# RWKV6 block on one core: one pool of six large tiles, squares of the head norm laid side by side, and a new planned order

## The chip, the core and the metric

The kernel runs on one core of a Trainium2 chip, all in float32. A core has the engines TensorE (PE: matmuls, and its weight loads PEld), VectorE (DVE), ScalarE (ACT), GpSimd (POOL) and SyncE (SP), which here issues nearly all DMAs. Each engine works through its own queue in order; engines wait for each other by semaphores. The metric is the device time of one execution in microseconds, the median of several runs.

## The reference

One RWKV6 block for B=32 sequences of L=128 tokens with E=512 channels, as H=32 heads of S=16. Cut to what matters:

```python
xn = _ln(x, ln1_w, ln1_b)
sx = _token_shift(xn, state[:, i1])                     # previous token minus this one
xxx = jnp.tanh((xn + sx * maa_x) @ maa_w1).reshape(b, l, 5, 1, EXTRA_MAA)
xxx = jnp.matmul(xxx, maa_w2).reshape(b, l, 5, E)
x5 = xn[:, :, None] + sx[:, :, None] * (maa_stack + xxx)  # five mixes: k, w, v, r, g
w = jnp.exp(-jnp.exp(time_decay + jnp.tanh(x5[:, :, 1] @ decay_w1) @ decay_w2))
r, k, v = x5[:, :, 3] @ Wr.T, x5[:, :, 0] @ Wk.T, x5[:, :, 2] @ Wv.T   # as (b, l, H, S)
g = jax.nn.silu(x5[:, :, 4] @ Wg.T)
def step(s, rkvw):                                      # scan over the 128 tokens, s: (b, H, S, S)
    a = k_t[:, :, :, None] * v_t[:, :, None, :]
    out = jnp.einsum('bhk,bhkd->bhd', r_t, u * a + s)
    return (a + w_t[:, :, :, None] * s, out)
a4 = att.reshape(b, l, H, S)                            # norm over each head's 16 values
att = ((a4 - m) * jax.lax.rsqrt(var + EPS)).reshape(b, l, E) * gn_w + gn_b
x = x + att * g @ Wo.T
xn2 = _ln(x, ln2_w, ln2_b)
xk, xr = xn2 + sx2 * ffn_maa_k, xn2 + sx2 * ffn_maa_r
return x + jax.nn.sigmoid(xr @ ffn_Wr.T) * (jnp.square(jax.nn.relu(xk @ ffn_Wk.T)) @ ffn_Wv.T)
```

## The kernel before

The 32 sequences are worked in nine groups, g0 to g8, of 2, 4, 4, 4, 4, 4, 4, 4 and 2. A group has a **front** (layernorm, token shift, the five mixes, the projections w, k, r, v, g), a **recurrence** and a **back** (head norm, gate, Wo, second layernorm, the FFN with its weights Fk, Fr, Fv). The work of several groups overlaps: TensorE does the front of a later group and the back of an earlier one while VectorE and GpSimd run the recurrence between them.

The order is not written in the program text. Each piece of work is a generator (a stream) that yields one operation at a time, with its engine, a guessed cost in microseconds, what it reads and writes, and the tiles it allocates. `Plan` (L101 to L207) runs when the kernel is built. It keeps a clock for each engine, takes of all streams those whose next operation can start within `EPSILON` (L49) of the earliest, and emits the one that is most due. Due times come from the table `DUE` (L53 to L77): for each kind of stream a start and an end in units of groups. So the guessed costs, `DUE` and `EPSILON` fix the order of each engine's queue, and the chip then follows that order whatever the true durations are. A tile name has a number of buffers (the spec, L228 to L242), and an allocation waits until a buffer of that name has been let go (`end=`).

The streams that matter here:

- Front: `front_mix` (L426; L439 and L442 make the shift, `mixed` L466 to L480 the five mixes with L470 and L475 on VectorE, L472 on GpSimd, after the L424 matmuls), `front_proj` (L510; the projections are the L407 matmuls, evicted by `k_out` L556, `r_out` L565 and `v_out` L576, and stored to DRAM by `store` L516, DMA L524), `front_gate` (L626; L642, L644, store L646), `front_state` (L648; its reduce L656).
- Recurrence, for each sequence in eight units: GpSimd multiplies k and v (L723) and adds pairs (L727); ACT copies the decay (L700) and the state (L711); VectorE scans (L742) and multiplies by r (L744); PE sums (L761). POOL makes the bonus (L772, L775, L779). VectorE adds both into y (L790). y has one buffer for a whole group; `rec_out` allocates it anew for a group's first sequence. vL, wL, rL, kL are loads from DRAM by SP (L679, L687), v2 too (L683).
- Back (L802): ACT squares y (L812), VectorE sums a head's 16 squares (L815), takes the reciprocal root in small steps (L818 to L825, three Newton steps) and scales y (L827). SP moves y in 16 DMAs into yc, the layout for matmuls (L835), loads the gate (L841); ACT applies the norm's weights (L843), VectorE the gate (L850), PE multiplies by Wo (L857). VectorE adds x and takes sums (L866), then layernorm in `layernorm_T` (L340: squares L364, L367, POOL L369, L371, L374, transposes L394, L384), the two mixes (L873, L876; L886, L888), Fk (L407 matmuls) with squared relu on ACT into kk (L913, L915), Fr (L923) with a sigmoid on ACT (L935), Fv (L938), VectorE (L928, L930) and the store of the result by SP (L932).

Large tiles of four by 512 floats a partition come under several names: "mx" (three buffers: the mixes, att), "ev" (one buffer: in turn the normalized x of both layernorms where they need one, the squares of y, yc and kk), "wch" and "pk" (one each, decay and k of the front). The two forms of the squares' layout are written in L810 to L815:

```python
sqv = sq.t.rearrange("p e n -> p (e n)")[:, 0 : S * nb * TC].rearrange("p (s m) -> p s m", s=S)
yv = y.t.rearrange("p s b c -> p s (b c)")[:, :, 0 : nb * TC]
nc.scalar.activation(sqv, yv, AF.Square)
...
nc.vector.tensor_reduce(m2, sqv.rearrange("p s m -> p m s"), AX.X, ALU.add)
```

Here m counts sequence and token (128 of them in a group of four), s the 16 values of a head. The squares lie as y does, s outermost, so the sum over s steps over m: 512 bytes in a group of four.

## Time and profile before

| | us |
|---|---|
| median of 3 runs | 1525.69 (1522.88, 1525.69, 1531.78) |
| the profiled execution | 1523.82, its span 1522.0 |
| busy PE | 1333.5 (88% of the span) |
| busy DVE | 1198.4 (79%) |
| busy POOL | 1084.2 (71%) |
| busy ACT | 633.7 (42%) |
| L815, the reduce of a group of four | 3.692 each, 7 of them |
| L812, the squares of a group of four | 1.911 each, 7 of them |
| L742 and L744, a unit of the recurrence on VectorE | 1.223 and 1.219 each, 256 of each |
| mean granted clock of TensorE | 0.932 |

The profile is one execution on the chip, taken by the hardware profiler. Its first part gives each engine's busy time. Its slices cut the span in 40 equal parts of 38 us; each digit is the busy share in tenths, and PEclk is the share of full speed that TensorE's clock was granted. A group line reads: line of the kernel, engine, operation, output tile <- input tiles, shapes, count, then busy us and mean ns of one, then idle time of the engine just before and what ended it. A line of waits reads: who waited, for whom, us in total, how often, longest. In a timeline, a line begins with start and duration in us, and the bracket gives idle time before it with the releaser. SPq stands for SP issuing DMAs.

### The profile page before, as it was taken

What the parts mean: (1) busy time and instruction counts of PE and PEld (TensorE: products, weight loads), DVE (VectorE), ACT (ScalarE), POOL (GpSimd) and SP (SyncE); (2) the same over time, 40 slices, a digit from 0 to 9 for tenths busy, and PEclk for the clock granted to TensorE, in tenths of its full rate; (3) what the DMA queues carried; (4) which work ended last, traced back from release to release, by engine and by line L of the source; (5) the groups of instructions that cost most, each with busy time, mean ns of one, the idle gap of its engine ahead of it and who ended that gap; (6) DMA issues with size and microseconds to landing.
All of it is one profiled execution on the core that took longest, in us unless ns stands there. A gap on an engine that the chain in (4) does not pass through costs nothing.

```text
span 1522.0 us, 18535 instructions
## 1 busy us (share of the span) xinstructions
PE 1333.5 (88%) x6060; PEld 606.3 (40%) x6060; DVE 1198.4 (79%) x1600; ACT 633.7 (42%) x1358; POOL 1084.2 (71%) x747
## 2 busy tenths in 40 slices
PE   8979988988899997999899998999899929955947
PEld 7734433442344333443344433443344506312413
DVE  4679788889788888779798898899888877886221
ACT  3433433453356422663255423653265314523413
POOL 3069569896889758795779867986898759977000
PEclk9989998998999998999999998999899969977979
DMA  5542736464655256553655366635565355535131
GB/s 186 166 111 106 216 105 189 147 173 127 187 157 162 84 151 185 166 159 103 187 180 175 86 177 214 186 98 155 167 184 161 102 141 152 160 88 161 39 89 65
DMA packets 292065, 222.52 MB, mean 146 GB/s; under 512 B 103936, under 2 KB 227840, under 8 KB 290816
## 3 DMA queue, kind: packets, MB, share of 16 engines
q1 hardware_dynamic: 291424, 221.10, 48.8%
q8 instruction: 48, 0.79, 0.2%
q14 instruction: 49, 0.40, 0.1%
q10 hardware_dynamic: 544, 0.23, 0.1%
HBM read 165.71 MB, written 47.19 MB: 140 GB/s over the span
## 4 chain that ended last, share of the span: by engine, by line
PE 58%; DVE 16%; issue 9%; SPq 6%; POOL 4%; DMA 4%; ACT 2%; POOLq 0%; DVEq 0%; ACTq 0%
PE ps L407 26%; PE ps L923 6%; PE ps L938 6%; PE ps L857 5%; PE acc L761 5%; SPq L835 4%; PE ps L424 4%; DVE sc L742 3%; DVE rm L744 3%; POOL am L723 2%; PE ps L413 2%; PE ps L394 1%; PE ps L450 1%; DVE mx L470 1%; DVE th L815 1%
## 5 line engine op out<-in xcount | busy, mean ns | idle before, releaser
L723 POOL TENSOR_TENSOR am<-vL,kL 128x1024 f32<-128x1024 f32 x256 | 604.0, 2360 | 70.9 <-DMA vL<-dv 53.2
L407 PE MATMUL ps<-mx,wt 128*128 128x512 f32 (+1 forms) x1440 | 591.5, 561 | 18.3 <-DVE mx L477 4.2
L407 PEld LDWEIGHTS ps<-mx,wt 128*128 128x128 f32 x1440 | 268.2, 193 | 304.8 <-issue 240.5
L742 DVE TENSOR_TENSOR_SCAN sc<-sc,a 128x512 f32<-128x512 f32 x256 | 313.1, 1223 | 31.0 <-POOL a L727 26.3
L727 POOL TENSOR_TENSOR a<-am 128x504 f32<-128x504 f32 x256 | 263.3, 1028 | 102.9 <-DVE sc L742 88.5
L744 DVE TENSOR_TENSOR rm<-sc,rL 128x1024 f32<-128x1024 f32 x256 | 312.2, 1219 | 14.4 <-PE acc L761 4.4
L700 ACT COPY sc<-wL 128x512 f32<-128x512 f32 x256 | 150.8, 589 | 257.6 <-DVE rm L744 250.7
L761 PE MATMUL acc<-rm,sel 128*32 128x256 f32 x2048 | 152.5, 408 | 61.5 <-DVE rm L744 61.4
L857 PE MATMUL ps<-wt,mx 128*128 128x512 f32 x256 | 123.3, 639 | 45.0 <-DVE mx L850 37.7
L472 POOL TENSOR_TENSOR mx<-mx,xnT 128x512 f32<-128x512 f32 (+1 forms) x96 | 105.2, 1113 | 68.6 <-DVE mx L470 68.1
L711 ACT COPY a<-st 128x8 f32<-128x8 f32 x256 | 51.5, 204 | 185.4 <-DVE sc L742 181.4
L761 PEld LDWEIGHTS acc<-rm,sel 128*32 128x32 f32 x2048 | 54.4, 112 | 171.6 <-DVE rm L744 82.4
L938 PE MATMUL ps<-wt,ev 128*128 128x512 f32 x256 | 117.6, 602 | 0.3 <-DVE mx L477 0.3
L923 PE MATMUL ps<-wt,mx 128*128 128x512 f32 x256 | 116.5, 598 | 0.6 <-ACT wch L539 0.4
L369 POOL TENSOR_TENSOR rstd<-rstd,mhalf 128x4 f32<-128x4 f32 (+1 forms) x18 | 17.1, 948 | 120.3 <-DVE rstd L367 119.9
L857 PEld LDWEIGHTS ps<-wt,mx 128*128 128x128 f32 x256 | 51.4, 206 | 114.6 <-issue 57.7
L424 PE MATMUL ps<-tha,w2p 64*128 64x512 f32 (+1 forms) x288 | 86.5, 624 | 10.0 <-DVE blk L644 4.3
L475 DVE SCALAR_TENSOR_TENSOR ps<-ps,vec,sx 128x512 f32<-128x512 f32 (+1 forms) x84 | 55.6, 662 | 23.6 <-PE ps L424 23.3
L938 PEld LDWEIGHTS ps<-wt,ev 128*128 128x128 f32 x256 | 46.7, 190 | 62.7 <-issue 50.7
L923 PEld LDWEIGHTS ps<-wt,mx 128*128 128x128 f32 x256 | 47.4, 190 | 60.7 <-issue 52.4
L470 DVE SCALAR_TENSOR_TENSOR mx<-ps,vec,sx 128x512 f32<-128x512 f32 (+1 forms) x96 | 65.5, 706 | 5.7 <-PE ps L424 5.7
L928 DVE SCALAR_TENSOR_TENSOR ps<-th,ps 128x512 f32<-128x512 f32 x32 | 22.1, 689 | 53.7 <-PE ps L938 37.0
(108 smaller groups left out, 1413.0 us busy)
## 6 DMA issues: line engine op xcount, KB each, us to landing
vL<-dv SPq DMA_DIRECT2D x128, 256.0 KB
x<-in_x SPq DMA_DIRECT2D x14, 1024.0 KB
wt<-in_wk SPq DMA_DIRECT2D x9, 1024.0 KB
wt<-in_wr SPq DMA_DIRECT2D x9, 1024.0 KB
wt<-in_wg SPq DMA_DIRECT2D x9, 1024.0 KB
wt<-in_wo SPq DMA_DIRECT2D x9, 1024.0 KB
wt<-in_fk SPq DMA_DIRECT2D x9, 1024.0 KB
wt<-in_fr SPq DMA_DIRECT2D x9, 1024.0 KB
```

Source lines behind the costliest of these rows:

```text
L407: nc.tensor.matmul(p[:, cols], lhsT=w[:, c, e * P : (e + 1) * P], rhs=xin[:, c, cols], start=(c == 0), stop=(c == NE - 1))
L424: nc.tensor.matmul(p[:, cols], lhsT=w[h, :], rhs=t[h, cols], start=True, stop=True)
L472: nc.gpsimd.tensor_tensor(bt(x5[:, f, cols]), bt(x5[:, f, cols]), row(xnT, f, 1, nb), ALU.add)
L700: nc.scalar.copy(sc.t, w[:, q : q + 1, :].to_broadcast([P, DH, T2]))
L723: nc.gpsimd.tensor_tensor(am.t, v[:, ds, :], k[:, q : q + 1, :].to_broadcast([P, DH, L]), ALU.mult)
L727: nc.gpsimd.tensor_tensor(a[:, :, 1:T2], am2[:, :, 0 : T2 - 1, 0], am2[:, :, 0 : T2 - 1, 1], ALU.add)
L742: nc.vector.tensor_tensor_scan(scf, scf, a.t.rearrange("p d n -> p (d n)"), 0.0, ALU.mult, ALU.add)
L744: nc.vector.tensor_tensor(pair(rm.t), sc.t.unsqueeze(3).to_broadcast([P, DH, T2, 2]), r2[:, q : q + 1, :, :].to_broadcast([P, DH, T2, 2]), ...
L761: nc.tensor.matmul(acc[j * H : (j + 1) * H, dh * DH * TC : (dh + 1) * DH * TC].rearrange("p (d c) -> p d c", c=TC), lhsT=sel, rhs=rm[:, :, ...
L857: nc.tensor.matmul(p.t, lhsT=att[:, c, b * L : (b + 1) * L], rhs=wot[:, c, :], start=(c == 0), stop=(c == NE - 1))
L923: nc.tensor.matmul(p.t, lhsT=xr[:, c, b * L : (b + 1) * L], rhs=frt[:, c, :], start=(c == 0), stop=(c == NE - 1))
L938: nc.tensor.matmul(p2.t, lhsT=kk[:, c, b * L : (b + 1) * L], rhs=fvt[:, c, :], start=(c == 0), stop=(c == NE - 1))
```

## The change

Three things change.

1. The names "ev", "wch" and "pk" go, and "mx" has six buffers in place of three. Six large tiles exist before and after; now any stream's large tile takes any of them. The allocations that named the three now name "mx" (in `layernorm_T`, `decay`'s first tile, the k projection, the squares, yc and kk).
2. The squares are written with a head's 16 values side by side: ACT's output now steps by 16 floats (64 bytes) from one value to the next, and the reduce reads adjacent values.
3. The planner gets other numbers: guessed costs of the stores (0.65 to 0.4), of L835 (2.6 to 2.9 for four DMAs) and of the second and third part of the bonus (0.65 to 0.72), another `EPSILON` and another table `DUE`. A mix is handed on when all four of its parts are made, in whatever order, in place of after the second half. No operation is added or taken out; the order of each queue is found anew.

```diff
--- before.py
+++ after.py
@@ -46,34 +46,34 @@
 LANDING = 2.0
 HOP = (0.2, 0.05, 0.05, 0.04, 0.08)
 ON_POOL = (2, 3, 4)
-EPSILON = 0.2067
+EPSILON = 0.1801
 
 
 OWN = {("mix", "first"), ("mix", "second"), ("mix", "last"), ("proj", "first"), ("proj", "second"), ("proj", "last"), ("weights", "first"), ("weights", "second"), ("gate", "first"), ("gate", "last"), ("back", "last"), ("back", "late"), ("back", "first")}
 DUE = {
-    "back": (0.998, 2.47),
-    "back_last": (-18.697, 1.751),
-    "back_late": (-42.476, -38.604),
-    "gate_last": (-7.141, -59.547),
-    "mix": (-2.339, -1.036),
-    "proj": (-1.408, -0.356),
-    "proj_second": (-1.35, 0.093),
-    "rec": (0.043, 8.058),
-    "weights": (-40.47, -7.934),
...
+    "back": (0.996, 2.471),
+    "back_last": (8.448, 60.13),
+    "back_late": (-31.956, -8.84),
+    "gate_last": (4.32, -85.128),
+    "mix": (-2.222, -1.037),
+    "proj": (-1.486, -0.286),
+    "proj_second": (-23.559, 1.139),
+    "rec": (0.042, 8.059),
+    "weights": (-72.983, -42.3),
...
 }
 
 
@@ -228,8 +228,8 @@
     spec = [
         (big, [P, GB, E], "x", 2), (big, [P, NE, E], "wt", 3),
         (big, [P, NE * GB, L + 1], "xnT", 1), (big, [P, NE, N], "sx", 1),
-        (big, [P, NE, N], "mx", 3), (big, [P, NE, N], "ev", 1), (big, [P, N], "blk", 4),
-        (big, [P, NE, N], "wch", 1), (big, [P, NE, N], "pk", 1), (big, [P, NE, N // 2], "pa", 1),
+        (big, [P, NE, N], "mx", 6), (big, [P, N], "blk", 4),
+        (big, [P, NE, N // 2], "pa", 1),
         (big, [P, Q, T2], "wL", 2), (big, [P, Q, L], "rL", 2), (big, [P, Q, L], "kL", 2), (big, [P, S, L], "vL", 2),
         (big, [P, S, TC], "v2", 1), (big, [P, S, TC + TC // 2], "bo", 1), (big, [P, GB, TC + TC // 2], "rk", 2),
         (big, [P, S, GB, TC], "y", 1), (big, [P, GB, Q, S], "st", 2),
@@ -358,7 +358,7 @@
             xh = None
             for b in bs:
                 if xh is None:
-                    (xh,) = yield Op(ACT, 0.83, r=[(src, b), (mv, "m")], w=[(0, b), (mv, ("v", b))], alloc=["ev"])
+                    (xh,) = yield Op(ACT, 0.83, r=[(src, b), (mv, "m")], w=[(0, b), (mv, ("v", b))], alloc=["mx"])
                 else:
                     yield Op(ACT, 0.83, r=[(src, b), (mv, "m")], w=[(xh, b), (mv, ("v", b))])
                 nc.scalar.activation(xh[:, b, :], src[:, b, :], AF.Square, bias=mv[:, b, 0:1],
@@ -476,7 +476,7 @@
                     yield Op(DVE, part(0.69, nb), r=[(p, None), (xnT, None)], w=[(x5, f)], end=[p])
                     nc.vector.tensor_tensor(bt(x5[:, f, cols]), bt(p[:, cols]), row(xnT, f, 1, nb), ALU.add)
                 d["mixed", m, f] = True
-            if i == 1:
+            if all(("mixed", m, f) in d for f in range(NE)):
                 d["x5", m] = x5
 
         for m in (1, 0, 3, 2, 4):
@@ -516,10 +516,10 @@
         def store(name, src, f, width, end):
             rows = slice(f * P, (f + 1) * P)
             if f == 0:
-                (d[name],) = yield Op(SP, 0.65, r=[(src, None)], w=[(0, f)], alloc=[name], xfer=part(1.2, nb), end=end)
+                (d[name],) = yield Op(SP, 0.4, r=[(src, None)], w=[(0, f)], alloc=[name], xfer=part(1.2, nb), end=end)
             else:
                 yield Op(SP, 0.0, need=lambda: name in d)
-                yield Op(SP, 0.65, r=[(src, None)], w=[(d[name], f)], xfer=part(1.2, nb), end=end)
+                yield Op(SP, 0.4, r=[(src, None)], w=[(d[name], f)], xfer=part(1.2, nb), end=end)
             t = src.t.rearrange("p b n -> p (b n)") if name == "dw" else src.t
             nc.sync.dma_start(out=d[name].t[rows, 0:width], in_=t[:, 0:width])
 
@@ -545,7 +545,7 @@
                 d["w", f] = True
 
         for i in range(2):
-            pp = yield Op(PE, PAIR * pe, r=[(dlo, None)], w=[(0, None), (1, None)], alloc=["ps", "ps"] + ([] if i else ["wch"]),
+            pp = yield Op(PE, PAIR * pe, r=[(dlo, None)], w=[(0, None), (1, None)], alloc=["ps", "ps"] + ([] if i else ["mx"]),
                           end=[dlo] if i else [])
             if i == 0:
                 wch = pp.pop()
@@ -578,7 +578,7 @@
             nc.scalar.copy(ev[:, cols], p[:, cols])
             yield from store("dv", ev, f, n, [ev])
 
-        for m, name, evict, take in ((0, "k", k_out, ["pk"]), (3, "r", r_out, ["pa"]), (2, "v", v_out, [])):
+        for m, name, evict, take in ((0, "k", k_out, ["mx"]), (3, "r", r_out, ["pa"]), (2, "v", v_out, [])):
             yield Op(PE, 0.0, need=lambda: ("x5", m) in d and ("w", name) in d and (m != 2 or "centered" in data[0]))
             x5, w = d["x5", m], d["w", name]
             late = []
@@ -770,11 +770,11 @@
             (bo,) = yield Op(POOL, 1.25, r=[(v2, None), (rk, None)], w=[(0, 0)], alloc=["bo"], port=True)
             one, two = bo[:, :, 0:TC], bo[:, :, TC : TC + TC // 2]
             nc.gpsimd.tensor_tensor(one, v2.t, rk[:, b : b + 1, 0:TC].to_broadcast([P, S, TC]), ALU.mult)
-            yield Op(POOL, 0.65, r=[(v2, None), (rk, None)], w=[(bo, 1)], port=True,
+            yield Op(POOL, 0.72, r=[(v2, None), (rk, None)], w=[(bo, 1)], port=True,
                      end=[v2] + ([rk] if b == SIZES[g] - 1 else []))
             nc.gpsimd.tensor_tensor(two, v2.t.rearrange("p s (m j) -> p s m j", j=2)[:, :, :, 0],
                                     rk[:, b : b + 1, TC : TC + TC // 2].to_broadcast([P, S, TC // 2]), ALU.mult)
-            yield Op(POOL, 0.65, r=[(bo, 1)], w=[(bo, 0)], port=True)
+            yield Op(POOL, 0.72, r=[(bo, 1)], w=[(bo, 0)], port=True)
             odd = one.rearrange("p s (m j) -> p s m j", j=2)[:, :, :, 1]
             nc.gpsimd.tensor_tensor(odd, odd, two, ALU.add)
             unit[i, "bo"] = bo
@@ -806,13 +806,13 @@
         yield Op(DVE, 0.0, need=lambda: "rec" in d and ("gate", NE - 1) in d)
         y = d["y"]
         wot = yield from weight(wo, lambda: g < 1 or ("back", "weights") in data[g - 1])
-        (sq,) = yield Op(ACT, part(1.9, nb), r=[(y, b) for b in bs], w=[(0, None)], alloc=["ev"])
-        sqv = sq.t.rearrange("p e n -> p (e n)")[:, 0 : S * nb * TC].rearrange("p (s m) -> p s m", s=S)
+        (sq,) = yield Op(ACT, part(1.9, nb), r=[(y, b) for b in bs], w=[(0, None)], alloc=["mx"])
+        sqv = sq.t.rearrange("p e n -> p (e n)")[:, 0 : S * nb * TC].rearrange("p (m s) -> p m s", s=S)
         yv = y.t.rearrange("p s b c -> p s (b c)")[:, :, 0 : nb * TC]
-        nc.scalar.activation(sqv, yv, AF.Square)
+        nc.scalar.activation(sqv.rearrange("p m s -> p s m"), yv, AF.Square)
         (small,) = yield Op(DVE, part(2.3, nb), r=[(sq, None)], w=[(0, None)], alloc=["th"], end=[sq])
         m2, yy, t = (small[:, i * P : i * P + nb * TC] for i in range(3))
-        nc.vector.tensor_reduce(m2, sqv.rearrange("p s m -> p m s"), AX.X, ALU.add)
+        nc.vector.tensor_reduce(m2, sqv, AX.X, ALU.add)
 
         yield Op(DVE, part(0.69, nb), w=[(small, None)], port=True)
         nc.vector.tensor_scalar(m2, m2, 1.0 / S, EPS, ALU.mult, ALU.add)
@@ -828,9 +828,9 @@
         yc = None
         for e in range(NE):
             if yc is None:
-                (yc,) = yield Op(SP, 2.6, r=[(y, None)], w=[(0, e)], alloc=["ev"], xfer=part(1.6, nb))
+                (yc,) = yield Op(SP, 2.9, r=[(y, None)], w=[(0, e)], alloc=["mx"], xfer=part(1.6, nb))
             else:
-                yield Op(SP, 2.6, r=[(y, None)], w=[(yc, e)], xfer=part(1.6, nb), end=[y] if e == NE - 1 else [])
+                yield Op(SP, 2.9, r=[(y, None)], w=[(yc, e)], xfer=part(1.6, nb), end=[y] if e == NE - 1 else [])
             for j in range(Q):
                 nc.sync.dma_start(out=yc[:, e, j * nb * TC : (j + 1) * nb * TC],
                                   in_=yv[j * H + e * HE : j * H + (e + 1) * HE])
@@ -907,7 +907,7 @@
             if e > 0:
                 p, f = late.pop(0), e - 1
                 if kk is None:
-                    (kk,) = yield Op(ACT, part(0.6, nb), r=[(p, None)], w=[(0, f)], alloc=["ev"], end=[p])
+                    (kk,) = yield Op(ACT, part(0.6, nb), r=[(p, None)], w=[(0, f)], alloc=["mx"], end=[p])
                 else:
                     yield Op(ACT, part(0.6, nb), r=[(p, None)], w=[(kk, f)], end=[p])
                 nc.scalar.activation(kk[:, f, cols], p[:, cols], AF.Relu)
```

"..." in the table stands for its other rows, which all change as well.

More of the change, by code (lines that the diff above doesn't have):

```diff
@@ L48 @@
 ON_POOL = (2, 3, 4)
-EPSILON = 0.2067
+EPSILON = 0.1801
 OWN = {("mix", "first"), ("mix", "second"), ("mix", "last"), ("proj", "first"), ("proj", "second"), ("proj", "last"), ("weights", "first"), ("weights", "second"), ("gate", "first"), ("gate", "last"), ("back", "last"), ("back", "late"), ("back", "first")}
 DUE = {
-    "back": (0.998, 2.47),
-    "back_first": (1.001, 2.842),
-    "back_last": (-18.697, 1.751),
-    "back_late": (-42.476, -38.604),
-    "center": (18.233, -20.613),
-    "gate": (5.025, -13.659),
-    "gate_first": (-1.137, -8.429),
-    "gate_last": (-7.141, -59.547),
-    "load": (-12.908, 19.489),
-    "mix": (-2.339, -1.036),
-    "mix_first": (1.194, 5.467),
-    "mix_last": (-11.53, -12.113),
-    "mix_second": (-1.924, -0.827),
-    "proj": (-1.408, -0.356),
-    "proj_first": (-2.407, -0.516),
-    "proj_last": (-9, 3.206),
-    "proj_second": (-1.35, 0.093),
-    "rec": (0.043, 8.058),
-    "state": (4.949, 0.89),
-    "warm0": (30.81, 39.251),
-    "weights": (-40.47, -7.934),
-    "weights_first": (16.502, 1.704),
-    "weights_second": (-22.418, -15.321),
+    "back": (0.996, 2.471),
+    "back_first": (1.379, -4.163),
+    "back_last": (8.448, 60.13),
+    "back_late": (-31.956, -8.84),
+    "center": (62.31, -1.713),
+    "gate": (4.863, -6.444),
+    "gate_first": (-0.774, -0.627),
+    "gate_last": (4.32, -85.128),
+    "load": (-6.043, -5.031),
+    "mix": (-2.222, -1.037),
+    "mix_first": (3.302, -4.409),
+    "mix_last": (-11.933, -1.779),
+    "mix_second": (-3.08, -0.718),
+    "proj": (-1.486, -0.286),
+    "proj_first": (-12.879, -4.085),
+    "proj_last": (-18.756, -7.148),
+    "proj_second": (-23.559, 1.139),
+    "rec": (0.042, 8.059),
+    "state": (0.71, -1.021),
+    "warm0": (2.516, 64.442),
+    "weights": (-72.983, -42.3),
+    "weights_first": (16.549, 19.386),
+    "weights_second": (-13.091, 8.817),
 }
```

## The prediction

> **What bounds the kernel now.** I read the page's slices first, then the waits of each engine, then the tail (1405 us to the end) engine by engine.
>
> ```profile
> PE   8979988988899997999899998999899929955947
> POOL 3069569896889758795779867986898759977000
> PEclk9989998998999998999999998999899969977979
> ```
>
> Up to slice 32 (38 us each) TensorE is the bound: one period of a middle group (L450 of one group to the next) is 163 to 179 us. From slice 33 on the fronts run out, PE falls to 2, later to 5, 5 and 4, and first the recurrence on POOL and VectorE sets the pace (POOL 9, 9, then 7, 7), then, with POOL empty, a chain that no engine's throughput bounds.
>
> ```profile
> PE ps L857 <- DVE mx L850: 21.2, 1, 21.2
> PE ps L394 <- ACT ev L374: 5.0, 2, 4.7
> ...
> 1453.40 0.60 ACT L935 ACTIVATE th<-ps 128x512 f32<-128x512 f32 x1 [6.27 <-PE ps L923]
> 1456.84 1.06 ACT L812 ACTIVATE ev<-y 128x1024 f32<-128x1024 f32 x1 [2.84 <-PE ps L938]
> 1469.26 0.57 ACT L843 ACTIVATE ps<-ev,vec 128x256 f32<-128x256 f32 x1 [11.37 <-DMA ev<-y]
> ...
> 1464.45 10.37 SPq L835 DMA_DIRECT2D ev<-y  x16
> ```
>
> These are the waits of PE after 1400 us and the timelines of ACT and SP. The last y (L790) is written at 1409.33, the last sums (L761) end at 1409.2. Yet its squares (L812) start at 1456.84, 47 us later, released by PE's last L938. The cause is in the names: L812 writes tile "ev", which has one buffer, and kk of the group before (g7) sits in it until that group's last L938. Only then follow L815, Newton's steps and L827 (to 1464.38), 16 transfers one after another on SP (10.37 us), L843, L850, and L857 at 1477.96: 21.2 us of idle PE, and a cold one afterwards (granted clock 0.59 between 1457 and 1478).
>
> **The change part by part**, against the profiled run (1523.82 us: span 1522.0 and 1.8 around it; 1.9 under the median 1525.69).
>
> *Squares side by side (L810 to L815).* No instruction is added or removed. L815 now reads 16 adjacent values in place of values 512 bytes apart; L812 now writes with a step of 64 bytes.
>
> ```profile
> L815 DVE TENSOR_REDUCE th<-ev 128x128 f32<-128x2048 f32 x7 | 25.8, 3692 | 0.0
> L656 DVE TENSOR_REDUCE stats<-st 128x16 f32<-128x256 f32 x7 | 2.8, 405 | 0.0
> L656 DVE TENSOR_REDUCE stats<-st 128x8 f32<-128x128 f32 x2 | 0.6, 279 | 0.0
> L812 ACT ACTIVATE ev<-y 128x2048 f32<-128x2048 f32 x7 | 13.4, 1911 | 0.0
> L812 ACT ACTIVATE ev<-y 128x1024 f32<-128x1024 f32 x2 | 2.1, 1053 | 2.8 <-PE ps L938 2.8
> ```
>
> L656 is a reduce over 16 adjacent values: (405-279)/128 = 0.98 ns an element and 0.15 us fixed. So 2048 elements: 2.17 us in place of 3.69, 1024: 1.16 in place of 1.90. That is 7 x 1.52 + 2 x 0.74 = 12.1 us of VectorE. In the chain of the whole run L815 stands with its 3.5 us four times (364, 548, 1220, 1351 us), elsewhere it is beside PE work. So 4 x 1.5 = 6, at most 12. L812 costs 0.84 ns an element; no row shows ACT writing 2048 elements strided. From below: ACT's small strided writes, L711 (8 elements 256 bytes apart, 204 ns) and L378 (16, 516 bytes apart, 209 ns), show no price for the step, so 0. From above: the step costs ACT what it costs VectorE's reads, 1.80-0.98 = 0.82 ns an element from L815 and L656, 1.7 us each, and eats the gain. I take 0, nearest to the ACT rows, less a little: **-5**, bounds -12 and +3.
>
> The Trainium skill (SBUF — State Buffer, section "Door 1: The DMA port swizzle") speaks against this edit: full bandwidth needs at least two hits in a 16-byte line, so float32 with a step of four or more pays at each element. The 0.8 ns on L815's read agrees; for ACT's write no row here shows it. By the rule, as an estimate, the sum of this edit would be about 0 instead of -5.
>
> *Six shared tiles, costs, due times, EPSILON.* None of these adds an instruction; they move buffers and the order of each engine's queue, fixed when the kernel is built. I compared both orders. In groups 2 to 5 TensorE's sequence is nearly the same, L812 still stands behind all L935 of the back before it, the L835s stay where they were. So the middle gains nothing but the reduce: **0**, bounds -2 and +2 us at each of 7 boundaries. Three places differ.
>
> *(a) Start.* The state loads go ahead of x on SP (two issues, about +1 us), k and r mixing is interleaved otherwise, the four v projections stand together, and the first vL may load some us earlier (before: v stored by 70.1, but the vL issue at 77.14 queued behind the gate's store; POOL's first L723 at 84.99). **-3**, bounds -6 and +1.
>
> *(b) When the last recurrence ends.* DVE's queue from g7's last y to the last L744 holds more in the new order: L876 x4 and L888 x4 (4 x 0.78 x 2 = 6.2 us) and some L928/L930 now stand before the last L744, and L815 to L827 as before. Against that, one stall goes:
>
> ```profile
> 1375.66 1.22 DVE L744 TENSOR_TENSOR rm<-sc,rL 128x1024 f32<-128x1024 f32 x1
> 1383.44 0.69 DVE L790 TENSOR_TENSOR y<-acc,bo 128x512 f32<-128x512 f32 x1 [6.56 <-DMA ev<-y]
> ```
>
> L790 of g8 writes y, whose one buffer is free when g7's 16 transfers have read it. They took 19 us after L827; only 12.6 us of VectorE work stood between L827 and this L790, now 26. The stall goes and nothing else is late there: the next wait is L850's, on the same transfers, as now. Also g7's L812 stands ahead of the last three L935s of g6 and L815 only 3 us of VectorE work after the last y (before: 11 us, with L815 at 1350.66, y at 1338.09). The same stall one group earlier (6.54 at 1252.12) has 16.6 us of work in place of 13.7 to hide it: -3. I sum rows along both DVE queues: g7's last y comes 5.4 us of work earlier, the stretch from it to the last L744 grows by 11.6 us of work, less 1.5 (reduce): -5.4 + 11.6 - 1.5 - 6.6 - 3 = -5. The L876s add a wait on VectorE: behind each stand recurrence steps, and PE's L761 waits for those. From the first L850 to the first L876 it took 28 us before (1384.2 to 1412), and only 25 us of VectorE work stand between them now: 2 to 3 us of waiting, up to 10 if each L876 waits (17.9 us for ACT in 14 places). Sum: -5 + 3 = **-2**, bounds -15 (the boundary chain 10 us earlier, no waits) and +10.
>
> *(c) The tail.* Before, from the last L761 (1409.2) to the span's end: 112.8 us. In the new order g7's four L407 groups (4 x 3.48 = 14 us) stand ahead of the last L761, L812 ahead of all four L935 of g7, and DVE runs L790, L815 to L827 before the first L928. After the last L761 PE has:
> - g7's L923 and L938, four pairs of 3.43 + 3.43: 27.5 us;
> - a gap before L857, below;
> - from L857's start to the end as before 1522.0-1477.96 = 44.0, less 2.0 because L857 now starts warm (16 took 8.81 us; 16 at L923's 3.43 per 8 take 6.86).
>
> The gap: the chain now runs beside the 27.5 us. L790 0.7, L812 1.06, L815 1.16, then Newton to L827's end (1464.38-1458.24-1.85 = 4.3) is done 7.3 us after the last L761. L835's 16 issues and L841 took 12.4, landing to L850 3: about 23 in all. But SP's new order mixes g7's four output stores (L932) between the L835s: 4, store, 8, store, 4 and one L841, store, three L841, store. The n-th store waits for L930 after the n-th L938, 8.3, 15.2, 22.0 us after the last L761. So the third store holds the last three gate loads until 22, they land by 25.5, and the fourth L850 waits anyway for the fourth L928/L930: 27.5 + 1.4 + 0.4. The gap is 2 us, not 21.2. Also behind the last store now: x and two weight loads of the last group, some 2 us later against L857 than before (issued 1476.80 to 1478.3); L866 needs x 7 us after L857's start and L407 its weight 16 after: covered, and if not, 2 us.
> Sum: 27.5 + 2 + 42 = 71.5 against 112.8: **-41**, bounds -43 and -28 (gap 15, if SP holds the L835s a pair longer twice).
>
> **Sum:** -5 + 0 - 3 - 2 - 41 = -51; 1522.0 - 51 + 1.8 = 1473 us.
>
> **Rivals.**
> 1. *The tail's chain stays late.* If L827 ends over 3 us later than I count, each block of L835 falls behind the next store, and a pair (6.9 us) is lost per block, two at most: +14. For it: 16 issues at 0.65 us fit the gaps of 6.9 us with little to spare. Against: the first four need only be issued before 8.3. 1487 us.
> 2. *The recurrence pays.* FFN work moved ahead of the last steps delays them: the L876s and L888s stall VectorE in order, the last sums move by +10, the start and the reduce give nothing: 1523.8 - 41 + 10 = 1493.
> 3. *The tail does not do what it says.* A front or back tile holds the sixth buffer, or L812 still waits for g7's L938; only the reduce and the start stay: 1516. Against it: no buffer is asked for by a front any more at that point.
> 4. *Slower: the shared pool at the boundaries.* Now kk, normalized x, squares, yc, mixes and projections take any of six buffers in the planned order; a tile of the back planned into a buffer that in truth comes free late stalls PE at each of the 7 middle boundaries, where a stretch of 40 us now loses 6.9 us of PE (33.1 busy, granted clock 0.93, 720 to 760 us). It decides from 51/7 = 7.3 us a boundary, a doubling of this lull. At 9 us: 1473 + 63 = 1536. For it: before, two idle stretches of 6 to 7 us at L424 and L857 already come from such waits (L424 <- L850 20.0 us in 3). Against: in groups 2 to 5 PE's order is nearly the same.
>
> **How the numbers follow.** Forecast (1455 to 1482) 0.55; rival 1 0.12, rival 2 0.12, rival 3 0.07, rival 4 0.09; better than forecast (boundary chains earlier everywhere) 0.05. Range: low end start -6, reduce -12, recurrence -12, tail -43: 1523.8 - 73 = 1451; the high end takes in rivals 1 and 2 and goes half-way from 2 to 3: 1506. About 0.5% (8 us) is what a measurement here can tell from no change; rival 3 lies at its edge. Faster 0.85, same 0.06, slower 0.09.
>
> **What would show it.** Right: L812 of the last group within 3 us of the last L761; no PE wait over 5 us before the last L857; from the last L761 to the end 70 to 75 us; L815 at 2.2 us, L812 at 1.9; no DVE wait at the last group's first L790; L450 of groups 2 to 5 spaced as before. Wrong: L812 at 3.5 us; SP's L835 in the tail waiting for L938; the last L744 later than 1410; a boundary where PE idles 10 us or more.

## The result and the profile after

The changed kernel takes 1475.66 us (median of 4 runs, 1474.92 to 1479.69), the kernel before 1526.24 on the same chip; the ratio is 0.967 with a 95% interval of 0.964 to 0.970. The forecast was 1473. The profiled execution has a span of 1477.9 us against 1522.0: 44.1 us less. The number was met; two of the steps behind it were not, and their errors cancelled, which is luck. What follows shows both.

The slices of the page after (36.9 us each), the same three rows as shown of before:

```profile
PE   7979998998799998999899998999899985676997
POOL 3069568997889779896889878896889957987300
PEclk8989999999889998999999999999999996787998
```

The 2 that stood in slice 33 of before is gone, and the last two slices are a 9 and a 7 where a 4 and a 7 stood: TensorE works to the end.

The tail of the changed kernel, from the timelines of ACT, SP and PE:

```profile
1406.90 0.63 ACT L915 ACTIVATE mx<-mx 128x512 f32<-128x512 f32 x1
1408.03 1.95 ACT L812 ACTIVATE mx<-y 128x1024 f32<-128x1024 f32 x1 [0.50 <-DVE y L790]
...
1415.55 2.69 SPq L835 DMA_DIRECT2D mx<-y  x4
1418.34 0.41 SPq L932 DMA_DIRECT2D out<-x  x1
1418.79 5.34 SPq L835 DMA_DIRECT2D mx<-y  x8
1424.23 0.41 SPq L932 DMA_DIRECT2D out<-x  x1
...
1431.31 3.60 PE L938 MATMUL ps<-wt,mx 128*128 128x512 f32 x8
1434.74 7.03 PE L857 MATMUL ps<-wt,mx 128*128 128x512 f32 x16
1446.41 0.48 PE L394 MATMUL ps<-ident,mx 128*128 128x128 f32 x1 [4.64 <-ACT mx L374]
```

L812 of the last group waits for the last y (0.5 us) and for nothing else. SP mixes L835 and L932 as forecast, and no store holds a transfer for long. L857 follows the last L938 without a gap (no bracket behind it) and runs warm, that is at a higher granted clock (1.00, before 0.80): 7.03 us in place of 8.81. From the end of the last L761 (1407.2) to the end it takes 70.7 us; 71.5 was forecast, 112.8 was before.

The squares and their reduce, by shape, after:

```profile
L812 ACT ACTIVATE mx<-y 128x2048 f32<-128x2048 f32 x7 | 26.1, 3722 | 0.4 <-DVE y L790 0.4
L815 DVE TENSOR_REDUCE th<-mx 128x128 f32<-128x2048 f32 x7 | 16.0, 2283 | 8.5 <-ACT mx L812 8.5
```

The reduce fell from 3692 to 2283 ns (2170 was forecast), but L812 rose from 1911 to 3722 ns, and VectorE now waits for it. The pair takes 6.00 us in place of 5.60.

**Where the 44.1 us came from.** Both are the profiled executions; that of the changed kernel is the slowest of its four. I cut both spans at the last y of a group (L790's timeline):

| from, to | before | after | difference |
|---|---|---|---|
| start to g1's last y | 345.7 | 347.1 | +1.4 |
| g1's to g2's | 175.1 | 167.5 | -7.6 |
| g2's to g3's | 179.8 | 164.4 | -15.4 |
| g3's to g7's | 637.5 | 634.4 | -3.1 |
| g7's to the end | 183.9 | 164.5 | -19.4 |

So 23 us come off between g1's last y and g3's, for which nothing but the reduce was forecast. The following lines, busy time by stretch (start, end, length, then PE, its weight loads, VectorE, ACT and POOL, each with its number of instructions, and the granted clock), show the stretches g1 to g2, g2 to g3, g3 to g4 and g4 to the end, first of before:

```profile
345.70:520.80 175.10, 162.67 (x705) 67.20 (x705) 151.09 (x194) 78.09 (x164) 138.75 (x93) 0.95 0.50 151
520.80:700.60 179.80, 165.04 (x699) 69.22 (x699) 148.96 (x189) 77.56 (x162) 135.90 (x92) 0.94 0.49 147
700.60:866.00 165.40, 157.16 (x697) 67.06 (x696) 144.03 (x188) 76.47 (x161) 134.70 (x91) 0.98 0.54 160
866.00:1522.00 656.00, 543.60 (x2391) 245.51 (x2389) 487.34 (x643) 260.24 (x555) 442.74 (x301) 0.90 0.47 137
```

and of after:

```profile
347.10:514.60 167.50, 152.75 (x672) 63.99 (x670) 140.89 (x182) 77.63 (x160) 138.02 (x92) 0.94 0.52 155
514.60:679.00 164.40, 157.79 (x697) 66.70 (x696) 144.45 (x187) 78.34 (x160) 136.95 (x91) 0.97 0.55 161
679.00:843.10 164.10, 156.96 (x697) 66.49 (x696) 144.03 (x187) 78.36 (x161) 136.95 (x91) 0.98 0.55 161
843.10:1477.90 634.80, 549.63 (x2391) 248.90 (x2389) 490.47 (x643) 267.87 (x555) 447.05 (x301) 0.92 0.48 141
```

A last y is not the same point of PE's queue in both kernels. From g1 to g2 the changed kernel has 33 matmuls less (672 against 705) and more idle PE (14.8 us against 12.4); it has done 36 of them before g1's last y (1608 against 1572), where its PE idles 32.8 us in place of 40.6. So this stretch is shorter because work of it was done earlier, in what was idle time of the start, though the table shows +1.4 there. At g2's last y both have done nearly the same matmuls (2280 and 2277), and the changed kernel is 6.2 us ahead. At g4's the same 2391 are left in both: from g2 to g4 it gains 16.7 us, from there to the end 21.2.

From g3 to g5 both kernels have the same period, 164 to 165 us. Before gets there one group later: its stretch g2 to g3 has as many matmuls as the next one (699 against 697), but 14.8 us of idle PE against 8.2, and the same matmuls take 165.0 us against 157.2, at a clock of 0.94 against 0.98. Half of the long stretch's idle time is one wait that the changed kernel doesn't have there:

```profile
PE ps L424 <- DVE pk L573: 7.5, 1, 7.5
```

Here 6.6 us more of idle PE went with 7.9 us more for the same matmuls, at the lower clock. That the idle time lowered the clock is read from the two together; no run separates them.

### The profile page after: what moved, and what is told of

The parts are those of the page before. It is cut to its first block, busy times and chain, and to the rows that moved or that the text cites. A ratio compares the mean times of both kernels' runs of the same rounds, so it can differ in the third digit from the quotient of the medians.

```text
span 1477.9 us, 18571 instructions
## 1 busy us (share of the span) xinstructions
PE 1331.5 (90%) x6060; PEld 607.9 (41%) x6060; DVE 1185.8 (80%) x1600; ACT 647.3 (44%) x1358; POOL 1094.6 (74%) x747
## 4 chain that ended last, share of the span: by engine, by line
PE 58%; DVE 16%; issue 8%; POOL 6%; SPq 5%; DMA 5%; ACT 3%; POOLq 0%; DVEq 0%; ACTq 0%
PE ps L407 26%; PE ps L923 6%; PE ps L938 6%; PE acc L761 5%; PE ps L424 5%; PE ps L857 4%; DVE sc L742 4%; POOL am L723 3%; SPq L835 3%; DVE rm L744 3%; PE ps L394 2%; POOL a L727 2%; DMA blk<-dgate 2%; PE ps L413 2%; PE ps L450 1%
## 5 line engine op out<-in xcount | busy, mean ns | idle before, releaser
L723 POOL TENSOR_TENSOR am<-vL,kL 128x1024 f32<-128x1024 f32 x256 | 605.3, 2365 | 45.9 <-DMA vL<-dv 17.1
L407 PE MATMUL ps<-mx,wt 128*128 128x512 f32 (+1 forms) x1440 | 590.3, 561 | 9.9 <-DVE mx L470 3.1
L407 PEld LDWEIGHTS ps<-mx,wt 128*128 128x128 f32 x1440 | 271.0, 195 | 290.5 <-issue 237.3
L744 DVE TENSOR_TENSOR rm<-sc,rL 128x1024 f32<-128x1024 f32 x256 | 311.9, 1218 | 14.6 <-PE acc L761 5.8
L761 PE MATMUL acc<-rm,sel 128*32 128x256 f32 x2048 | 153.0, 409 | 90.4 <-DVE rm L744 90.1
L472 POOL TENSOR_TENSOR mx<-mx,xnT 128x512 f32<-128x512 f32 (+1 forms) x96 | 115.2, 1216 | 68.0 <-DVE mx L470 67.7
L761 PEld LDWEIGHTS acc<-rm,sel 128*32 128x32 f32 x2048 | 52.2, 111 | 204.2 <-DVE rm L744 96.7
L711 ACT COPY a<-st 128x8 f32<-128x8 f32 x256 | 51.8, 203 | 180.0 <-DVE sc L742 179.3
L938 PE MATMUL ps<-wt,mx 128*128 128x512 f32 x256 | 122.7, 624 | 7.6 <-DMA wt<-in_fv 7.6
L857 PE MATMUL ps<-wt,mx 128*128 128x512 f32 x256 | 122.5, 639 | 3.7 <-ACT th L935 3.7
L923 PE MATMUL ps<-wt,mx 128*128 128x512 f32 x256 | 116.5, 598 | 0.0
L424 PE MATMUL ps<-tha,w2p 64*128 64x512 f32 (+1 forms) x288 | 81.4, 602 | 6.1 <-ACT mx L539 4.2
L857 PEld LDWEIGHTS ps<-wt,mx 128*128 128x128 f32 x256 | 51.9, 206 | 73.4 <-issue 59.0
L938 PEld LDWEIGHTS ps<-wt,mx 128*128 128x128 f32 x256 | 48.5, 197 | 73.1 <-issue 53.1
L923 PEld LDWEIGHTS ps<-wt,mx 128*128 128x128 f32 x256 | 47.5, 190 | 61.1 <-issue 52.8
L384 ACT ACTIVATE xnT<-ps,vec 128x512 f32<-128x512 f32 (+1 forms) x72 | 52.5, 729 | 15.8 <-PE ps L394 15.7
```

Of the source, the lines that this page charges most:

```text
L407: nc.tensor.matmul(p[:, cols], lhsT=w[:, c, e * P : (e + 1) * P], rhs=xin[:, c, cols], start=(c == 0), stop=(c == NE - 1))
L424: nc.tensor.matmul(p[:, cols], lhsT=w[h, :], rhs=t[h, cols], start=True, stop=True)
L472: nc.gpsimd.tensor_tensor(bt(x5[:, f, cols]), bt(x5[:, f, cols]), row(xnT, f, 1, nb), ALU.add)
L723: nc.gpsimd.tensor_tensor(am.t, v[:, ds, :], k[:, q : q + 1, :].to_broadcast([P, DH, L]), ALU.mult)
L744: nc.vector.tensor_tensor(pair(rm.t), sc.t.unsqueeze(3).to_broadcast([P, DH, T2, 2]), r2[:, q : q + 1, :, :].to_broadcast([P, DH, T2, 2]), ...
L761: nc.tensor.matmul(acc[j * H : (j + 1) * H, dh * DH * TC : (dh + 1) * DH * TC].rearrange("p (d c) -> p d c", c=TC), lhsT=sel, rhs=rm[:, :, ...
```

## The experiments

Ratios below are to the kernel before on the same chip, with 95% intervals; the changed kernel stands at 0.967 (0.964 to 0.970).

**1. The changed kernel with the old squares (e1).** The queues keep their order, since the planner's costs for L812 and L815 are the same in both kernels.

```diff
-sqv = (...)rearrange("p (m s) -> p m s", s=S)
-nc.scalar.activation(sqv.rearrange("p m s -> p s m"), yv, AF.Square)
-nc.vector.tensor_reduce(m2, sqv, AX.X, ALU.add)
+sqv = (...)rearrange("p (s m) -> p s m", s=S)
+nc.scalar.activation(sqv, yv, AF.Square)
+nc.vector.tensor_reduce(m2, sqv.rearrange("p s m -> p m s"), AX.X, ALU.add)
```

> The changed kernel with the squares laid out as before (ACT writes adjacent values, the reduce reads with a step); every queue keeps the order of the changed kernel. Theory (the layout is no gain): in the changed kernel L812 takes 3.72 us and L815 2.28, in all 6.00, before 1.91 and 3.69, in all 5.60; undone, the pair is 0.40 us shorter at each of up to 9 places, so 0 to 4 us faster than the changed kernel: 1472 to 1476 us. Rival (VectorE, 80% busy, is what counts, so the 1.4 us a reduce that it saves are worth it, the 5 us of the prediction): undone, 5 us slower, 1481 us.

Measured: 1474.65 us, ratio 0.966 (0.963 to 0.970). No gain of the new layout is seen. The two intervals together tell only some 7 us from nothing, so the rival's 5 us are not excluded by this run; they are by experiment 3.

**2. ACT reads with a step in place of writing with one (e3).**

```diff
-nc.scalar.activation(sqv.rearrange("p m s -> p s m"), yv, AF.Square)
+nc.scalar.activation(sqv, yv.rearrange("p s m -> p m s"), AF.Square)
```

> The changed kernel, but ACT goes through the squares in the order in which they are to lie: it reads y with a step and writes adjacent values; the reduce reads adjacent values; order of all queues as in the changed kernel. Theory W (the price sits in ACT's strided write): L812 goes back to about 1.9 us, L815 stays at 2.28, so 1.8 us less at each boundary, up to 9 of them on the path: 1460 to 1470 us. Rival RW (a step costs a read as much as a write): L812 stays near 3.7 us and the time at 1475 us.

Measured: 1477.48 us, ratio 0.969 (0.966 to 0.971): no difference. The groups of e3, by shape:

```profile
L812 ACT ACTIVATE mx<-y 128x2048 f32<-128x2048 f32 x7 | 26.5, 3786 | 0.4 <-DVE y L790 0.4
L815 DVE TENSOR_REDUCE th<-mx 128x128 f32<-128x2048 f32 x7 | 16.0, 2285 | 9.4 <-ACT mx L812 9.4
```

Here a read with a step of 512 bytes costs ACT what a write with one of 64 bytes costs, 3786 against 3722 ns. Theory W falls, RW stands: the step is paid on whichever side it lies.

**3. The kernel before with the new squares alone (e2).** The edit of experiment 1 the other way round.

> The kernel before with the new layout of the squares alone; order, tiles and due times as before. Theory (the layout is no gain): L812 3.72 us, L815 2.28, so 0.4 us longer at each boundary: 1526 to 1530 us. Rival (the reduce's saving on VectorE counts): 5 us faster, 1521 us.

Measured: 1526.37 us against 1526.63, ratio 0.999 (0.997 to 1.001). The interval leaves room neither for a gain of 5 us nor for a loss of more than 2.2.

**4. The kernel before with two free tiles for the last norm (e5).**

```diff
-alloc=["ev"]                                  # the squares
+alloc=["ev" if g < NG - 1 else "wch"]
-alloc=["ev"]                                  # yc
+alloc=["ev" if g < NG - 1 else "pk"]
```

> The kernel before, where only the last group's squares and yc go into tiles that are free by then (those named wch and pk) in place of ev; up to the last Fk matmuls of group g7 every queue stays as it was, after that the order is found anew and is nearly that of the changed kernel's tail (L835 and L932 mixed on SP). Theory (the last group's norm waited for kk in ev): the 21.2 us gap before the last L857 falls to 2 to 5, L857 runs warm (2 us less): 19 to 21 us faster, about 1505 us; L812 within 3 us of the last y. Rival 1 (SP's stores hold the L835s, the gap only halves): about 1515. Rival 2 (what gains in the tail is that Fk work is put ahead of the last L761, not the tile): about 1526, no change.

Measured: 1504.95 us, ratio 0.986 (0.983 to 0.989): 21.7 us faster. PE's waits at L857 from the last L761 to the end, in e5:

```profile
PE ps L857 <- DVE mx L850: 1.9, 2, 1.8
```

The 21.2 us before the last L857 have become 1.9, although Fk of g7 stays behind the last L761. Rival 2 falls. L812 was not early, against what was expected of it: it started at 1430.9, 21 us after the last y, behind g7's L913 and L915 on ACT. Its chain still fits beside the 27.5 us of L923 and L938.

**5. The changed kernel with the old wait in the tail (e4).**

```diff
-need=lambda: "rec" in d and ("gate", NE - 1) in d
+need=lambda: "rec" in d and ("gate", NE - 1) in d and (g < NG - 1 or "done" in data[g - 1])
 ...
+        d["done"] = True                      # at the end of a group's back
```

> The changed kernel, where only the last group's back may not begin until g7's back has been issued whole; up to then all queues stay as they are, and the tail gets the order of before: L812 after g7's four L935, 16 L835s after its four L932. Theory (a norm that waits for g7's last L938 costs its chain): the gap before the last L857 comes back with 19 to 21 us, and L857 runs cold (2 us): 1496 to 1499 us. Rival (the tail's gain comes from Fk put ahead of the last L761, which stays): 1476 to 1480.

Measured: 1500.86 us, ratio 0.984 (0.981 to 0.987), 25 us slower than the changed kernel. PE's wait at L857 from the last L761 to the end, in e4:

```profile
PE ps L857 <- DVE mx L850: 20.6, 1, 20.6
```

The gap is back, and up to that point the kernel runs as the changed one does (g7's last y at 1311.1, there 1313.4). Experiments 4 and 5 show it from both sides: a norm of the last group that waits until g7's kk is done with (e4 makes it wait for g7's whole back) costs 22 to 25 us of the 51.

**6. Tiles and due times apart (e6, e7).** e6 is the kernel before with the tiles shared, e7 the changed kernel with the tiles apart:

```diff
-"mx", 3 ... "ev", 1 ... "wch", 1 ... "pk", 1        # e6: from this
+"mx", 6                                             # to this, and the six allocations with it
```

> The kernel before with the six tiles shared; due times, costs, EPSILON and layout of the squares as before. The order that comes out has g7's and g8's L812 ahead of the L935s of the back before, as in the changed kernel, and is that of before in most other places; Fk of g7 stays behind the last L761. Theory T (the tiles decide the tail, the due times the middle): the tail's gap goes as with the two free tiles, and g7's norm begins some us earlier: 1498 to 1506 us, with the groups up to g6 timed as before (g6's last y at about 1189). Rival D (the gain is that of the new due times alone): 1526. Rival M (sharing also frees the boundaries of the middle groups): under 1490.

> The changed kernel with ev, wch and pk given back as tiles of their own and three mx; due times, costs, EPSILON and the new layout stay. The order that comes out has the tail of before (L812 behind all L935 of the back before, Fk of g7 behind the last L761). Theory T: the middle keeps what the new due times gave (g6's last y 22 us earlier than before, at about 1167), the tail is that of before (about 113 us after the last L761): 1503 to 1510 us. Rival D (due times alone): 1476. Rival M (the due times pay only with shared tiles): 1526.

Measured: e6 1518.00 us, ratio 0.994 (0.992 to 0.996); e7 1545.19 us, ratio 1.011 (1.009 to 1.014).

| | separate tiles | shared tiles |
|---|---|---|
| old due times | 1526.4 | 1518.0 |
| new due times | 1545.2 | 1475.7 |

"New due times" stands for all of the third change, the new layout with it. None of the three theories was right in both. The parts don't add: tiles alone give -8, due times alone +19, together -51. Theory T was right of the gap before the last L857 (under 2 us in e6, 21.0 in e7), but not of the tail's length: after the last L761 e7 takes 142 us, where T said about 113, and from g7's last y to the end e6 takes 171.5 us and e7 207.6 (before 183.9). It was wrong of the middle: e7, with the new due times, has lost all of the middle's gain (g6's last y at 1190, before 1189, after 1167).

**7. Which tile (e9, e10).** The changed kernel with ev alone apart (e9: five mx, one ev), or wch alone (e10: five mx, one wch).

> The changed kernel, where only ev is a tile of its own again (five mx, one ev for normalized x, squares, yc and kk); the rest as changed. The order that comes out has the tail of the kernel with all tiles separate. Theory E (ev alone makes the loss of the separate tiles): 1530 to 1548 us, g6's last y at 1180 to 1190, the gap before the last L857 at about 21 us. Rival W (wch and pk cost in the middle, ev only in the tail): the middle as changed (g6's last y at 1167) and only the tail longer: 1500 to 1510.

> The changed kernel, where only wch is a tile of its own again (five mx, one wch); the rest as changed; the order of some 300 rows on TensorE's queue moves, the tail keeps its shape. Theory E (ev alone makes the loss): 1474 to 1485 us. Rival W (wch costs in the middle): 1490 to 1500. Rival S (any other order loses): 1490 and more.

Measured: e9 1537.61 us, ratio 1.006 (1.004 to 1.008); e10 1490.13 us, ratio 0.975 (0.972 to 0.977). PE's waits in the tail of e9:

```profile
PE ps L857 <- DVE mx L850: 21.1, 1, 21.1
```

ev brings the gap back, as in e7; wch doesn't, but loses 14 us all the same between the medians and 12 between the profiled spans, and these 12 are there by g2's last y (526.9 against 514.6), where PE's order differs. So it is not ev alone.

**8. The order by itself (e8, e12).** EPSILON changed and nothing else: 0.2067 in the changed kernel (e8), 0.1801 in the kernel before (e12).

```diff
-EPSILON = 0.1801
+EPSILON = 0.2067
```

> The changed kernel with EPSILON of before (0.2067 for 0.1801); tiles, due times, costs and layout as changed. It is a control for the order: many operations change places on every queue, the tail keeps its shape (L812 ahead of g7's L935s, Fk of g7 ahead of the last L761). Theory E (what costs is the one buffer ev; the exact order costs little): 1476 to 1488 us. Rival S (the table fits one set of numbers only, and any other order loses what the separate tiles lost): 1495 us or more.

> The kernel before with EPSILON of the changed kernel (0.1801 for 0.2067): the control of the order on the other side; tiles, due times, costs and layout as before, the tail keeps its shape. Theory S (a table of due times fits one set of numbers, and any other order loses in the first groups, where the recurrence comes into step): 1540 us or more, g3's last y at 710 or later. Rival (the changed EPSILON is itself a gain, the order of before was a poor one): 1500 to 1520. Rival (orders near each other differ by a few us only): 1522 to 1532.

Measured: e8 1501.63 us, ratio 0.982 (0.980 to 0.984), 26 us slower than the changed kernel; e12 1553.56 us, ratio 1.017 (1.012 to 1.021), 26 slower than before. The two stretches of the middle, g1's last y to g3's, less two periods of 164.3 us, give what it costs to come into step:

| kernel | g1 to g3, us | over two periods |
|---|---|---|
| changed | 331.9 | 3 |
| changed, wch apart (e10) | 344.9 | 16 |
| changed, all apart (e7) | 347.5 | 19 |
| changed, ev apart (e9) | 347.8 | 19 |
| changed, other EPSILON (e8) | 351.8 | 23 |
| before | 354.9 | 26 |
| before, shared (e6) | 356.5 | 28 |
| before, other EPSILON (e12) | 363.4 | 35 |

The kernels in which PE's and VectorE's order is that of the changed one (e1: 331.3, e3: 330.5, and up to the tail e4: 330.5 and e11: 333.3) have its 2 to 5 us. Each of the others, with another order, loses 16 us or more there, whichever tiles it has. Since g1's last y is no even point of the work, g3's last y alone is the safer measure: 679.0 us in the changed kernel, 691.6 (e10) to 704.5 (e6) in the others. Rival S holds for the changed kernel: the middle's gain is this one order, and every edit tried that moves the order loses it. In e12 the stretch is 8.5 us longer than before; most of its loss lies later (from g7's last y to the end 203.6 us, before 183.9), so there Theory S is right of the loss and not of its place, and its g3 was at 703.5, not 710.

**9. Gates first (e11).** In the last two groups L841 goes ahead of L835.

```diff
+        if g >= NG - 2:
+            for f in range(NE):
+                yield from load_gate(f)          # L841, before the 16 L835
```

> The changed kernel, where the last two groups load their gates (L841) ahead of the 16 transfers of y (L835) in place of behind them. In the changed kernel g7's L850 waits 4.5 us for its gate, behind v loads and a store on SP, and the back of g7 sets the end from there on. Theory (g7's back is the chain that sets the end): 3 to 5 us faster, 1471 to 1473 us. Rival (PE's order holds L857 behind g6's L923 and L935 anyway, 3.7 us at L857): 1475 to 1477.

Measured: 1479.23 us, ratio 0.967 (0.964 to 0.969), no gain. In e11 the lines below L830 stand ten lower: L867 is L857, L933 is L923, L948 is L938. PE in e11:

```profile
1346.46 2.84 PE L867 MATMUL ps<-wt,mx 128*128 128x512 f32 x6
...
1398.19 3.70 PE L933 MATMUL ps<-wt,mx 128*128 128x512 f32 x8
...
1430.23 4.54 PE L867 MATMUL ps<-wt,mx 128*128 128x512 f32 x6 [1.92 <-DVE mx L860]
1435.81 4.56 PE L867 MATMUL ps<-wt,mx 128*128 128x512 f32 x10 [1.04 <-DVE mx L860]
```

g7's Wo starts 13 us earlier than in the changed kernel (1346.5 against 1359.3) and its L923 9 us earlier (1398.2 against 1407.2), and the end doesn't move. What is late next is the last group: its last y comes 4 us later (1411.0), and from there its own norm, transfers and gate need 24 us to the last L860 (1435.3). The theory falls. The rival (1475 to 1477) is nearer in its number, but its reason fails too, since g7's Wo did start earlier. In this run g7's back and g8's recurrence and norm end together. That both would have to be shortened is argued from that; no run tried it.

## Why the prediction was right, and where it was not

**The tail's cause (right).** One buffer ev held by kk, a wait of 21.2 us, hidden beside L923 and L938 once the squares have a tile of their own: e5 and e4 show it alone, 22 and 25 us; forecast were 19 for the gap and 2 for the cold clock. The gap's detail was right too: forecast 2 us, measured 0; the stores on SP held nothing that mattered. Rivals 1 and 3 did not come. Of rival 2 the cost came by another way (next paragraph).

**"*(b)* -2" and "*(c)* -41" (right against the last L761, wrong as a sum).** The last L761 ends at 1407.2, 2 us earlier, the tail behind it is 42.1 us shorter, as forecast. But the start, the reduce and (b) were to bring the last L761 forward by 10 us in all. They were to bring g7's last y forward by 16.4 (3, 5, 5.4 and 3), and it came 24.7 us earlier, mostly by the middle, for which 0 stood. From g7's last y to the last L761 the changed kernel needs 93.8 us, before 71.1: +22.7, where my terms (11.6 - 1.5 - 6.6 and 3 of waits) give +6.5. The failed step is "I sum rows along both DVE queues". It saw VectorE's queue, where the last L744 does come 7.6 us earlier, and not PE's. The stretch from g7's last y to the end of the last L761, of before and of the changed kernel:

```profile
1338.10:1409.20 71.10, 37.33 (x182) 13.39 (x180) 55.55 (x65) 20.67 (x44) 52.28 (x35) 0.72 0.37 106
1313.40:1407.20 93.80, 72.56 (x265) 29.70 (x265) 67.33 (x79) 37.45 (x69) 55.78 (x37) 0.84 0.36 108
```

and the end of the latter:

```profile
1395.67 10.57 PE L407 MATMUL ps<-mx,wt 128*128 128x512 f32 x24 [1.27 <-DVE mx L888]
1406.17 1.07 PE L761 MATMUL acc<-rm,sel 128*32 128x256 f32 x16
```

PE is busy for 35.2 us more there and idle for 12.5 less. Fk of g7 was put ahead of the last L761, so the last L761 waits behind Fk, 6 us after VectorE had its input ready (L744 from 1399.3 to 1400.5). I counted the 14 us of L407 as gained in (c) and nearly nothing as paid for them in (b). The rest of the 83 matmuls more are the 16 transposes L394 of g7, ahead of the last L761 as well, and 35 of g6's L923 and L938, which the kernel before had done ahead of g7's last y. From g7's last y to its first L923 it took 91.1 us before (1338.1 to 1429.2) and takes 93.8 now: Fk changed sides of the last L761, and the way to the first L923 became no shorter. From g7's last y to the end the change gives 19.4 us; steps (b) and (c), counted from the same point, had given 34.5 (-41 + 6.5). PE's idle time does fall by 35.1 us there (66.1 to 31.0), but its busy time grows by 15.7, with 416 matmuls in place of 381: g6's 35. Rival 2 had the last sums 10 us later by waits on VectorE, with no gain from start and reduce. The last sums came 16 us later than summed, by PE's queue; without the 23 us of the middle the time would, as an estimate, have been 1499 us, nearer to that rival's 1493 than to 1473.

**The stalls before L790 (one right, one wrong).** VectorE's first L790 of g7 and of g8, after:

```profile
1233.45 0.69 DVE L790 TENSOR_TENSOR y<-acc,bo 128x512 f32<-128x512 f32 x1 [7.32 <-DMA blk<-dgate]
...
1361.37 0.67 DVE L790 TENSOR_TENSOR y<-acc,bo 128x512 f32<-128x512 f32 x1
```

The stall of g8 is gone, as forecast; that of g7 is 7.3 us in place of 6.5, where 3 less was forecast. L850 of g7 now waits 4.5 us for its gate at 1353.1; I had it wait there for the transfers of y.

**"So the middle gains nothing but the reduce: 0, bounds -2 and +2 us at each of 7 boundaries" (wrong).** It gained 23 us in g1 to g3, some 6 of them by work done earlier, in idle time of the start, as shown above, and 3 after. I had seen that one of the periods of before was 179 us and the others 161 to 165, and did not ask what the long one lost: 6.6 us of idle PE and 7.9 of slower matmuls more than the next. And "nearly the same" of PE's sequence was judged over groups 2 to 5 together. L450 of groups 2 to 5 was to be spaced as before; its spaces were 161, 161 and 179 us and are 124, 185 and 164, with g3's front 31 us earlier (300.7 against 331.9). The boundary lulls were not doubled, so rival 4 did not come: PE waited 6.1 to 7.1 us at one L424, and waits 6.8 to 6.9 us at two L761 together now. One of the signs of being wrong did come, a boundary with 10 us of idle PE (10.3 before the L761 at 1235.3), but 9.8 and 9.6 us stood there before.

**"Squares side by side: -5" (wrong, size 0).** The reduce was sized well (2.28 us, forecast 2.17). ACT's write was taken at no price from L711 and L378, with 8 and 16 elements: at 0.9 ns an element more, 16 elements cost 14 ns more, little beside some 200 ns. L378's two sizes, 193 ns for 8 elements and 209 for 16, would have given 2 ns an element and a hint of the price. The upper bound (VectorE's price for a step, 1.7 us) was nearly the truth: 1.81 us. Of the bounds I took the row of the same engine, and should have taken the one of the same size. L812 at 3.5 us was named as a sign of being wrong, and it took 3.7. The page SBUF — State Buffer of the Trainium skill (section "Door 1: The DMA port swizzle") states that each access that crosses to a new 16-byte line pays a penalty. These runs agree, for ACT's write (1.81 us more) and in e3 for its read (1.9 more), and the estimate of 0 by that page was nearer than mine.

**"(a) Start: -3" (small).** The first L723 starts at 83.1 in place of 85.0; by g1's last y it shows as +1.4, with 36 matmuls more done; by g2's, with the work even, 6.2 us are gained, so the start gave more than forecast and by another way.

**The sum.** Forecast -51, measured -44.1 in the profiled runs and -50.6 between the medians. Against the profiled runs, what follows g7's last y was taken 15 us too good, the squares 5, the start 4 and the order between g3 and g7 5; the middle was 23 too poor: -51 + 15 + 5 + 4 + 5 - 23 = -45, the measured 44 but for rounding. The range was added up loosely: its low end took 12 us of (b), whose own bound was 15, and half-way from rival 2 to 3 is 1504, not 1506.

**What stays open.** Which places of the order spare the middle groups their idle time is not shown: the kernels that lose there (e7 to e10, e12) differ from the changed one in many places at once. e6 loses as much from g2 to g3 as before (180.8 us) though its wait at L424 for L573 is 0.6 us there in place of 7.5, so that wait alone is not the cause. Shown is that the gain goes with the order, and that it lies in coming into step, not in the steady period.

## What to carry to other kernels

Where a chain at the end waits for a buffer, look at what its tile shares a name with, and give only that tile another home: e5 has 22 of the 51 us with two words changed. When work is moved past a milestone, measure from a point at which both kernels have the same work left (here g4's last y, with 2391 matmuls to go; g7's last y has 35 more behind it in the changed kernel), or the same work is counted as gained on one side and not as paid on the other. This planned order is tuned to its exact numbers: a changed EPSILON cost 26 us on either kernel, so a part of such a change judged with the order found anew says little about the part, and edits that leave the order alone (e1 to e3) or change it only behind a point (e4, e5) say much.

## What the runs showed of the hardware

With the steps of these runs a float32 element costs ACT's Square twice as much, read or written: from the two sizes of L812, 0.84 ns an element adjacent (1911 and 1053 ns), 1.72 written 64 bytes apart (3722 and 1964), 1.75 read 512 bytes apart (3786 and 1996). VectorE's reduce pays 1.75 ns an element with a step of 512 bytes (3692 and 1896) and 1.04 without (2283 and 1220). So the change of layout between these two engines only moved the price from the one to the other.
